# Four graph-attention layers on one core: which unit turns the tiles, and in what order the first and last groups are written

## The chip, the core and the metric

The kernel runs on one core of one Trainium2 chip. A core has five engines that run side by side and wait for each other by semaphores: TensorE (PE; weight loads are listed as PEld), VectorE (DVE), ScalarE (ACT), GpSimd (POOL) and SyncE (SP), which here only issues DMAs. Sixteen DMA engines move data between the chip's memory and the on-chip memory. The metric is the device time of one execution in microseconds; lower is better.

## What is computed

64 graphs of 256 nodes with 256 features pass through four layers. Each layer is an attention over the graph's edges, and after each one `x = layernorm(x + layer(x))`. Cut to what matters here:

```python
# layer 0: 4 heads of 64, masked softmax, output projection, layer norm
attn = softmax(where(adj == 0, NEG, q @ k.T * 64 ** -0.5))
out = layernorm((attn @ v) @ Wo.T + bo) * gamma + beta
# layer 1: 8 heads of 32; q = k = v = layernorm(x)*gamma1+beta1, then an MLP 256-1024-256
x = x + softmax(masked(z @ z.T * 32 ** -0.5)) @ z
out = x + gelu((layernorm(x) * gamma2 + beta2) @ W1 + b1) @ W2 + b2
# layer 2: one head; e = leaky_relu(s1 + s2), softmax over the edges, times h @ W
# layer 3: e_k = leaky_relu((h * a_k) @ h.T) chosen by the edge's type, softmax, times h
```

A matrix product needs the summed index on the partitions, so node-first tiles have to be turned (transposed) before several of the products: `x` before q and k, `z` before layer 1's scores, `yT` before the MLP, `n2` before layer 2 and `n3` before layer 3. Layer 1's head outputs come out feature-first and have to be turned back before they are added to node-first `x`.

## The kernel before, in words

`usual_input` (from L416) computes the usual case; at the end a flag says whether the input allowed it, and the general `any_input` runs only if not. All arithmetic is in f32. The 64 graphs are worked in 32 groups of two. Every group is a set of eleven generators, called threads (`threads_of`, L1066): `a` loads and masks, makes q, k, v, layer 0's scores, exponentials and products (L651); `u0`, `u1`, one for each graph, do the rest of layer 0 (L752); `z0`, `z1` turn z (L791); `b` is layer 1's attention (L798); `w0`, `w1` its sums and second norm (L837); `c` the first product of the MLP with Gelu (L866); `o0`, `o1` the second product and layers 2 and 3 (L911).

A thread is cut into steps by `yield`. `PLACES` gives each step of each thread a place in units of one group's period; group g adds g. The steps of all groups are sorted by place (L1075) and issued in that order, and the class `InOrder` (L432) keeps each engine's instructions in just this order. Engines still run apart and wait only for data and buffers. So the order of the work is written out, engine by engine, and an instruction that waits holds up all that stand behind it on its engine, SyncE's queue of DMAs among them. `prepare` (L992) works out constants from the weights; one of its parts is issued after each step from `PREPARE` = 2 on. As every call goes through the helper `issue`, the profile puts nearly all instructions on its line, L444, and they are told apart by their tiles.

**Turning a tile.** `flipped` (L620) has two ways. With `direct`, four TensorE transposes of 128x128 go into PSUM and ScalarE copies them out. Otherwise `put` (L599) writes the tile to a buffer `rows` in the chip's memory with two DMAs, `get` (L606) reads it back in four DMAs as `blk`, so that 32x32 blocks stand where they belong, and `turn_blocks` (L614) turns each block with one VectorE transpose. Before the change z, yT, n2 and n3 of all groups go by DMA. `x` is also read by DMA as blocks, `turned` (L487), and turned by VectorE. Layer 1's head outputs `oT` are turned by four TensorE transposes for each graph in `thread_w` (`pm<-ident,oT` in the profile).

**Layer 0's sums.** `products` in `thread_a` (L727) multiplies the exponentials with v and, with a matrix of ones, makes the softmax sums `pz`, 128x256: each head's sum of each node stands in 32 equal rows. VectorE takes the reciprocal of the whole tile into `zs`; ScalarE passes over it once more to add the reciprocals up into `r_0`, which the check at the end needs. `thread_u` writes four rows of `zs` (one for each head) to the chip's memory (`lines`), reads them back spread over the partitions (`rr`), multiplies `oT` with them and goes on to the product with `woT`.

The order of loads at the start: adjacency of the first group, its `turned` blocks, `x`; the weights for q, k, v on ScalarE's queue; the others on SyncE's as part of `prepare`.

Of the kernel before, what the change touches and what calls it, by code (L numbers as in the profile page):

```python
# [8 lines left out]
F32 = mybir.dt.float32  # L9
# [28 lines left out]
SCZ = SCB = SCN = True  # L38
B2 = False
BUFS = dict(t=6, q=3, k=2, v=5, y=4, z=5, xb=5, both=4, xn=6, mask=3, e=5, x0=2, turned=1, blk=3, oT=2, zs=2, rr=2, xT=1, qT=1, kT=1)  # L40
PLACES = {
    "a": (0.0000, 0.1609, 0.3936, 0.4188, 1.1456, 1.2085, 1.2135, 1.2684, 1.2684, 1.3083, 1.3187, 1.3922,
        1.4411, 1.4550, 1.5065, 1.5209, 1.5704, 1.6232, 1.7014, 1.7014, 1.7046, 1.7114, 1.7202, 1.7320,
        1.7466,),
    "u0": (1.7845, 1.8009, 1.8519, 1.8867, 1.9096, 1.9241, 1.9842, 1.9890, 2.0092, 2.1939,),
    "u1": (1.8219, 1.8841, 1.9554, 2.0080, 2.0097, 2.0560, 2.0570, 2.0890, 2.1304, 2.1482,),
    "z0": (2.0380, 2.0800, 2.1517, 2.1771,),
    "z1": (2.1482, 2.1622, 2.2237, 2.2465,),
    "b": (2.2092, 2.2292, 2.2314, 2.2463, 2.2634, 2.2658, 2.2687, 2.2708, 2.2708, 2.2724, 2.2924, 2.3032,
        2.3032, 2.3033, 2.3118, 2.3118, 2.3245, 2.3249, 2.3345, 2.3549,),  # L50
    "w0": (2.3066, 2.3129, 2.3245, 2.3779, 2.4390, 2.5803, 2.5997, 2.6786,),
    "w1": (2.4161, 2.4739, 2.4805, 2.4835, 2.6234, 2.6271, 2.6419, 2.7222,),
    "c": (2.7903, 2.8184, 2.8324, 2.9205, 2.9215, 2.9612, 3.0404, 3.0557,),
    "o0": (3.0690, 3.0731, 3.1620, 3.1894, 3.2073, 3.2439, 3.2672, 3.3855, 3.4219, 3.4420, 3.4926, 3.5020,
        3.5298, 3.5520, 3.5620, 3.5786, 3.6006, 3.7170, 3.7358, 3.7614, 3.8702, 3.9115, 3.9399, 3.9768,
        4.0664, 4.2516, 4.2674, 4.2795, 4.2936, 4.3095, 4.3669, 4.3935, 4.6003, 5.1336,),
    "o1": (3.0936, 3.2383, 3.2389, 3.2476, 3.3303, 3.5076, 3.5188, 3.5336, 3.5988, 3.6912, 3.7420, 3.7551,
        3.7936, 3.8172, 3.8298, 3.8317, 3.8389, 3.8773, 3.9738, 3.9793, 4.0267, 4.0708, 4.0708, 4.0809,
        4.1171, 4.5258, 4.5963, 4.6712, 4.6849, 4.7832, 4.8010, 4.9844, 4.9844, 5.1775,),
}  # L60
PREPARE = 2

# [357 lines left out]
def usual_input(ctx: ExitStack, tc: tile.TileContext, a: dict, out: bass.AP, flag: bass.AP):  # L420
# [56 lines left out]
    edges = const.tile([P, B // G], F32, name="edges")  # L477
    r_0 = const.tile([P, B], F32, name="r_0")
    r_3 = const.tile([P, B, QB], F32, name="r_3")
    last = const.tile([P, B, QB], F32, name="last")  # L480
# [6 lines left out]
    def load_x(g):  # L487
        turned = None
        if FX:
            turned = new(io, [P, NC, T // 32, 32], F32, "turned")  # L490
            rows = a["x"][g * G:(g + 1) * G].rearrange("b n d -> (b n) d")
            parts = rows.rearrange("(t i) (c k j) -> k i c t j", i=32, c=NC, j=32)
            for k in range(P // 32):
                for c in range(NC):
                    SP.dma_start(turned[32 * k:32 * k + 32, c], parts[k, :, c])
        x0 = new(io, [P, TB, D], F32, "x0")
        SP.dma_start(x0, a["x"][g * G:(g + 1) * G].rearrange("b (q p) d -> p (b q) d", p=P))
        return x0, turned
# [3 lines left out]
    def load(queue, to, of):  # L502
        if queue:
            queue.dma_start(to, of)
        else:
            later.append((to, of))
# [15 lines left out]

    def load_all(src, name, at=None):

        t = const.tile([P, D], F32, name=name) if at is None else setup[:, at:at + D]
        load(None, t, src.unsqueeze(0).to_broadcast([P, D]))
        return t

    first = load_edges(0), load_x(0)
    wqT = load_rows("L0_gnn_WqT", D, ACT)  # L530
    wkT = load_rows("L0_gnn_WkT", D, ACT)
    bq = load_column(a["L0_gnn_bq"], D, "bq", ACT)
    bk = load_column(a["L0_gnn_bk"], D, "bk", ACT)
    wvT = load_rows("L0_gnn_WvT", D, ACT)
    woT = load_rows("L0_gnn_WoT", D)
    bv = load_column(a["L0_gnn_bv"], D, "bv")
# [5 lines left out]
    load(None, a12, a["L2_gnn_a"].rearrange("(s f) o -> o s f", s=2).to_broadcast([P, 2, D]))  # L542
    beta0 = load_all(a["L0_gnn_beta"], "beta0")
    gamma0 = load_all(a["L0_gnn_gamma"], "gamma0")
# [74 lines left out]

    def flipped(src, direct, name):  # L620

        if direct:
            pt = new(ps_m, [P, QB, NC, P], F32, "pm", 4)
            for q in range(QB):
                for c in range(NC):
                    transpose(pt[:, q, c, :], src[:, q, c * P:(c + 1) * P], ident)
            yield
            dst = new(act, [P, QB, NC, P], F32, "t")
            ACT.copy(dst, pt)
            return dst  # L630
        rows = put(src)
        yield
        blk = get(rows)
        yield
        return turn_blocks(blk)
# [15 lines left out]
    def thread_a(g, s):  # L651
# [18 lines left out]
        xT = new(act, [P, NC, T], F32, "xT")  # L670
        if FX:
            DVE.transpose(xT.rearrange("p c t -> p (c t)"), turned.rearrange("p c t j -> p (c t j)"))
        else:
            pts = []
            for c in range(NC):
                pt = new(ps_m, [P, T], F32, "pm", 4)
                for t in range(TB):
                    transpose(pt[:, t * P:(t + 1) * P], s["x"][:, t, c * P:(c + 1) * P], ident)
                ACT.copy(xT[:, c, :], pt)
# [30 lines left out]
        def scores(i):  # L710
            ps = []
            for c in range(NC):
                p = new(ps_s, [P, 2, QB * N], F32, "ps", 2)
                for kc in range(QB):
                    for h in range(2):
                        r = h * 64
                        matmul(p[:, h, kc * N:(kc + 1) * N], kT[r:r + 64, c, i * N + kc * P:i * N + (kc + 1) * P],
                               qT[r:r + 64, c, i * N:(i + 1) * N], start=True, stop=True)
                ps.append(p)
            yield  # L720
            es = []
            for c in range(NC):
                es.append(exp_of(ps[c], 64 ** -0.5, mask[:, i, :], None, c, 0))
                yield
            return es

        def products(i, es):  # L727
# [6 lines left out]
            pz = new(ps_m, [P, N], F32, "pm", 4)  # L734
            for kc in range(QB):
                for h in range(4):
                    matmul(pz[32 * h:32 * h + 32, :], ones[:, 0:32], es[h // 2][:, h % 2, kc * N:(kc + 1) * N],
                           start=kc == 0, stop=kc == QB - 1)
# [3 lines left out]
            zs = s["zs", i] = new(act, [P, N], F32, "zs")  # L742
            DVE.reciprocal(zs, pz)
            ACT.activation(pz, zs, AF.Copy, accum_out=r_0[:, g * G + i:g * G + i + 1])
            yield
# [6 lines left out]
    def thread_u(g, s, i):  # L752
# [3 lines left out]
        SP.dma_start(lines.rearrange("c h n -> (c h) n"), zs[0:P:32, :])  # L756
        yield
        for h in range(2):
            SP.dma_start(rr[h * 64:h * 64 + 64, :, :], lines[:, h, :].unsqueeze(0).to_broadcast([64, NC, N]))
# [31 lines left out]
    def thread_z(g, s, i):  # L791
        zT = s["zT", i] = yield from flipped(s["z", i], not FZ, "z")
        yield
# [43 lines left out]
    def thread_w(g, s, i):  # L837
        r, oT = s["sums", i], s["o", i]
        DVE.reciprocal(r, r)
        pt = new(ps_m, [P, QB, D], F32, "pm", 4)  # L840
        for q in range(QB):
            for c in range(NC):
                transpose(pt[:, q, c * P:(c + 1) * P], oT[:, c, q * P:(q + 1) * P], ident)
        yield
        x2 = new(act, [P, QB, D], F32, "y")
# [13 lines left out]
        yield  # L859
        yield from flip_to(s, "yT", i, xb, not FY)  # L860

    def flip_to(s, name, i, src, direct):
        s[name, i] = yield from flipped(src, direct, name)
        yield
# [46 lines left out]
    def thread_o(g, s, i):  # L911
# [15 lines left out]

        xT = yield from flipped(x, not FN2, "n2")
        yield
# [25 lines left out]

        xT = yield from flipped(x, not FN3, "n3")
        yield
# [34 lines left out]
    def prepare():  # L992

        for to, of in later[:-2]:
            SP.dma_start(to, of)
        for _ in range(4):
            yield

# [67 lines left out]
    def threads_of(g):  # L1066
# [4 lines left out]
                "o0": thread_o(g, s, 0), "o1": thread_o(g, s, 1)}  # L1071

    preparing = prepare()
    groups = [threads_of(g) for g in range(B // G)]
    plan = sorted((g + t, g, n, k) for g in range(B // G) for n, ts in PLACES.items() for k, t in enumerate(ts))  # L1075
    for turn, (_, g, name, k) in enumerate(plan):
        next(groups[g][name], END)
        if turn >= PREPARE:
            next(preparing, END)
    assert all(next(t, END) == END for ts in groups for t in ts.values())  # L1080

# [52 lines left out]
```

## Time and profile before

| what | us |
|---|---|
| median of 3 runs (lowest to highest) | 2550.32 (2550.2 to 2553.7) |
| the profiled execution | 2552.08 |
| its span | 2550.3 |
| TensorE busy | 2461.3 (97%) |
| VectorE busy | 2013.9 (79%) |
| ScalarE busy | 1604.5 (63%) |
| GpSimd busy | 675.0 (26%) |
| one group's period in the middle (second group's adjacency load to the next, 1499.87 to 1575.69) | 75.8 |

The profile is of one execution. Busy time is the union of an engine's instructions; matmul ends are modelled and neighbours overlap, so what a TensorE instruction costs is best read from start to start. The span is the time from the first to the last instruction of the program; the executed time is a little longer. A line of a group reads: line, engine, operation, output<-inputs, shapes, count, then busy time and mean ns of one, then the idle time of the engine ahead of these instructions and what ended it.

### The profile page before, as it was taken

The numbers are of one execution on the slowest core, as the hardware profiler recorded it, in microseconds if no ns is written. First come the engines' busy times: TensorE is split into PE (matmuls) and PEld (weight loads), VectorE is DVE, ScalarE is ACT, GpSimd is POOL, SyncE is SP. The second block draws the span as 40 slices with busy tenths as digits, with TensorE's granted clock in tenths as the row PEclk, the third lists the DMA queues.
The fourth block names the chain that finished last, engine by engine and source line by source line (L and its number), as shares of the span: only waits on it lengthen the run. The fifth ranks groups of instructions, "written<-read, shape, count | busy, mean of one in ns | idle before, by whom it ended". The sixth has DMA issues, their size and how long they took to land.

```text
span 2550.3 us, 48577 instructions
## 1 busy us (share of the span) xinstructions
PE 2461.3 (97%) x16424; PEld 1834.3 (72%) x16424; DVE 2013.9 (79%) x6060; ACT 1604.5 (63%) x2687; POOL 675.0 (26%) x1807
## 2 busy tenths in 40 slices
PE   5699999999999999999999999999999999999995
PEld 3377777777777777777777777777777777777764
DVE  3677788888888887887888887888878888888764
ACT  2456666676666666666666666667666666666652
POOL 0122222232232222233222232223223223223311
PEclk8799999999999999999999999999999999999987
DMA  5333444444444444444444444444434444443332
GB/s 132 67 86 86 92 100 91 93 100 91 94 99 91 94 99 96 96 92 94 95 96 96 94 92 95 94 92 100 95 90 99 92 96 97 96 92 87 67 71 51
DMA packets 929360, 234.55 MB, mean 92 GB/s; under 512 B 728784, under 2 KB 928720, under 8 KB 929104
## 3 DMA queue, kind: packets, MB, share of 16 engines
q1 hardware_dynamic: 927744, 230.59, 40.6%
q8 instruction: 132, 2.16, 0.4%
q14 instruction: 124, 1.02, 0.1%
q10 hardware_dynamic: 1360, 0.79, 0.1%
HBM read 138.69 MB, written 84.15 MB: 87 GB/s over the span
## 4 chain that ended last, share of the span: by engine, by line
PE 79%; DVE 6%; POOL 6%; ACT 4%; issue 2%; DMA 1%; SPq 1%; POOLq 0%; ACTq 0%; DVEq 0%
PE pm L444 69%; PE ps L444 10%; POOL rstd L444 3%; DVE y L444 3%; DVE st L444 2%; POOL ve L444 2%; ACT L444 2%; ACT z L444 1%; POOL nm L444 1%; ACT hT L444 1%; SPq L444 1%; DVE mv L444 1%; DVE e L444 0%; DMA blk<-rows 0%; DMA L_gnn_W<-in_L_gnn_W 0%
## 5 line engine op out<-in xcount | busy, mean ns | idle before, releaser
L444 POOL TENSOR_SCALAR ve<-mv 128x2 f32<-128x2 f32 x448 | 163.4, 365 | 1750.7 <-DVE mv L444 1208.0
L444 PE MATMUL pm<-L_gnn_W,hT 128*128 128x256 f32 x2048 | 477.9, 384 | 5.3 <-ACT hT L444 5.3
L444 PE MATMUL pm<-t,L_gnn_W 128*128 128x256 f32 x2048 | 463.0, 379 | 1.4 <-DVE t L444 1.4
L444 PEld LDWEIGHTS pm<-L_gnn_W,hT 128*128 128x128 f32 x2048 | 379.6, 190 | 87.7 <-ACT hT L444 25.0
L444 ACT ACTIVATE e<-ps 128x1024 f32<-128x1024 f32 x384 | 374.1, 1018 | 102.8 <-PE ps L444 100.4
L444 PEld LDWEIGHTS pm<-t,L_gnn_W 128*128 128x128 f32 x2048 | 389.1, 190 | 54.9 <-DVE t L444 1.8
L444 DVE SCALAR_TENSOR_TENSOR e<-e,mask 128x256 f32<-128x256 f32 x1024 | 361.1, 419 | 58.8 <-ACT e L444 58.8
L444 POOL TENSOR_TENSOR rstd<-ve,mhalf 128x2 f32<-128x2 f32 (+1 forms) x384 | 305.7, 796 | 31.9
L444 ACT ACTIVATE xn<-y,nm,rstd 128x256 f32<-128x256 f32 x256 | 139.8, 594 | 199.5 <-POOL xn L444 155.0
L444 DVE BATCH_NORM_STATS2 st<-y 128x6 f32<-128x256 f32 x640 | 236.9, 412 | 5.6
L444 ACT ACTIVATE hT<-pm,b 128x512 f32<-128x512 f32 x256 | 167.7, 682 | 51.3 <-PE pm L444 48.9
L444 DVE STREAM_TRANSPOSE t<-blk 128x512 f32<-128x512 f32 x256 | 178.8, 698 | 22.7 <-DMA blk<-rows 22.6
L444 PE MATMUL ps<-t 32*128 32x256 f32 x2048 | 158.2, 405 | 14.3 <-ACT t L444 12.5
L444 ACT ACT_TABLE_LOAD x127 | 162.9, 1283 | 5.7 <-issue 3.5
L444 DVE TENSOR_TENSOR e<-e,mask 128x1024 f32<-128x1024 f32 x128 | 152.1, 1211 | 12.4 <-ACT e L444 12.4
L444 PEld LDWEIGHTS ps<-t 32*128 32x128 f32 x2048 | 101.7, 186 | 67.3 <-ACT t L444 23.1
L444 PE MATMUL pm<-xn,q 128*128 128x257 f32 x512 | 135.6, 389 | 0.0
L444 PE MATMUL pm<-L_gnn_WoT,oT 128*128 128x256 f32 x512 | 125.0, 388 | 9.3 <-DVE oT L444 9.2
L444 PE MATMUL pm<-v,q 128*128 128x260 f32 x512 | 127.4, 393 | 5.1 <-DVE q L444 3.6
L444 PE MATMUL pm<-e,z 128*32 128x256 f32 x2048 | 131.7, 384 | 0.1
L444 ACT COPY v<-pm 128x259 f32<-128x259 f32 (+1 forms) x192 | 84.1, 438 | 75.4 <-PE pm L444 71.4
L444 DVE SCALAR_TENSOR_TENSOR y<-pm,r,xn 128x256 f32<-128x256 f32 x256 | 123.9, 484 | 9.0
(126 smaller groups left out, 4162.3 us busy)
## 6 DMA issues: line engine op xcount, KB each, us to landing
blk<-rows SPq DMA_DIRECT2D x1024, 64.0 KB
rows<-xn SPq DMA_DIRECT2D x256, 128.0 KB
adj<-in_adj SPq DMA_DIRECT2D x32, 512.0 KB
turned<-in_x SPq DMA_DIRECT2D x256, 64.0 KB
x<-in_x SPq DMA_DIRECT2D x32, 512.0 KB
rr<-lines SPq DMA_DIRECT2D x128, 128.0 KB
rows<-z SPq DMA_DIRECT2D x128, 128.0 KB
rows<-xb SPq DMA_DIRECT2D x128, 128.0 KB
```

Source lines behind the costliest of these rows:

```text
L444: ins = call(*args, **kw)
```

## The change

It has four parts.

1. `FO`: `thread_w` writes `oT` to `rows` with two DMAs, reads it back with `get` and turns the blocks with VectorE, in place of TensorE's four transposes. It adds one step to `w0` and `w1`.
2. `SM`: ScalarE only copies `pz` to `zs`; the four rows go to `lines` as before, come back as a 32x32 tile `few`, are inverted there, written out to a second `lines`, and spread from that. The adding up for `r_0` is done on the small tile. It adds three steps to `u0` and `u1`.
3. `DIRECT`: in the first group (0) `x` and `z` are turned by TensorE, and the sums take the old way; in the last (31) `yT`, `n2`, `n3` and the head outputs are turned by TensorE. `x` of the first group is now loaded ahead of its adjacency, and `beta0` on ScalarE's queue.
4. The order: `PLACES` has new numbers throughout; the first 500 and the last 484 of the steps follow two written lists, `FIRST` and `LAST`; the parts of `prepare` are issued after seven named steps.

`PA` is false and changes nothing. `any_input` is as before. The order of each engine moves accordingly; ScalarE's has 65 table loads where it had 127.

```diff
+FO = True
+PA = False
+SM = True
+DIRECT = {0: ('x', 'z', 'sm'), 31: ('yT', 'n2', 'n3', 'o')}
...
-PREPARE = 2
+PREPARE = (8, 16, 30, 60, 75, 85, 95)
+FIRST = (
+    "a0a0a0a0a0a0a0a0a1a1a1a1a1a0a0a0a0a0a0a0a0a0a0a0a0a0a0a0U0U0U0a1a1U0a0a0U0U0u0u0a2a2U0U0U0u0u0u0u0u0U0U0U0u0"
...
-        if FX:
+        if FX and "x" not in DIRECT.get(g, ()):
...
-    first = load_edges(0), load_x(0)
+    x_first = load_x(0)
+    first = load_edges(0), x_first
...
+    beta0 = load_all(a["L0_gnn_beta"], "beta0", queue=ACT)
...
-        if direct:
+        if direct or name in DIRECT.get(g, ()):
...
             ACT.copy(dst, pt)
+            if not direct:
+                yield
             return dst
...
-            DVE.reciprocal(zs, pz)
-            ACT.activation(pz, zs, AF.Copy, accum_out=r_0[:, g * G + i:g * G + i + 1])
+            if SM and "sm" not in DIRECT.get(g, ()):
+                ACT.copy(zs, pz)
+            else:
+                DVE.reciprocal(zs, pz)
+                ACT.activation(pz, zs, AF.Copy, accum_out=r_0[:, g * G + i:g * G + i + 1])
...
+        elif SM:
+            few = new(small, [32, 32], F32, "few", 4)
+            SP.dma_start(few, lines.rearrange("c h (a b) -> (c h a) b", b=32))
+            yield
+            DVE.reciprocal(few, few)
+            ACT.activation(few_out[0:32, :], few, AF.Copy, accum_out=r_0[0:32, g * G + i:g * G + i + 1])
+            yield
+            lines = new(dram, [NC, 2, N], F32, "lines", 4)
+            SP.dma_start(lines.rearrange("c h (a b) -> (c h a) b", b=32), few)
+            yield
...
-        DVE.reciprocal(r, r)
-        pt = new(ps_m, [P, QB, D], F32, "pm", 4)
-        for q in range(QB):
+        if FO and "o" not in DIRECT.get(g, ()):
+            DVE.reciprocal(r, r)
+            rows = new(dram, [QB, NC, P, P], F32, "rows", 8)
             for c in range(NC):
-                transpose(pt[:, q, c * P:(c + 1) * P], oT[:, c, q * P:(q + 1) * P], ident)
-        yield
+                SP.dma_start(rows[:, c].rearrange("q p j -> p q j"), oT[:, c, :].rearrange("p (q j) -> p q j", q=QB))
+            yield
+            blk = get(rows)
+            yield
+            pt = turn_blocks(blk).rearrange("p q c j -> p q (c j)")
...
-        for to, of in later[:-2]:
+        for to, of in later[:3]:
             SP.dma_start(to, of)
-        for _ in range(4):
-            yield
+        yield
+        for to, of in later[3:-2]:
+            SP.dma_start(to, of)
+        yield
...
-    plan = sorted((g + t, g, n, k) for g in range(B // G) for n, ts in PLACES.items() for k, t in enumerate(ts))
-    for turn, (_, g, name, k) in enumerate(plan):
+    plan = [(g, n) for _, g, n in sorted((g + t, g, n) for g in range(B // G) for n, ts in PLACES.items() for t in ts)]
+    head, tail = written(FIRST, 0), written(LAST, B // G - 8)
+    for turn, (g, name) in enumerate(head + plan[len(head):len(plan) - len(tail)] + tail):
         next(groups[g][name], END)
-        if turn >= PREPARE:
+        if turn in PREPARE:
             next(preparing, END)
```

In `FIRST` and `LAST` a letter names the thread (`U`, `u` are `u0`, `u1`; `O`, `o` are `o0`, `o1`, and so on) and the digit the group, counted from 0 and from 24.

## The prediction

> **What bounds the kernel now.** I read the table of windows first, since an average over the span hides stages. Its columns are the stretch, its length, each engine's busy time, then the granted TensorE clock, the DMA share and GB/s.
>
> ```profile
> 0.00:100.00 100.00, 54.55 (x278) 33.22 (x282) 43.74 (x115) 27.78 (x44) 9.77 (x29) 0.76 0.47 112
> 100.00:250.00 150.00, 145.04 (x1017) 103.90 (x1013) 112.75 (x349) 89.74 (x143) 34.07 (x76) 1.00 0.37 81
> 250.00:2300.00 2050.00, 2044.97 (x13854) 1529.62 (x13844) 1690.33 (x5086) 1356.58 (x2272) 569.08 (x1515) 1.00 0.43 95
> 2300.00:2450.00 150.00, 146.78 (x1010) 110.84 (x1009) 123.20 (x383) 94.07 (x158) 42.36 (x115) 0.99 0.34 75
> 2450.00:2551.00 101.00, 69.95 (x280) 56.74 (x279) 43.90 (x129) 36.30 (x72) 19.70 (x74) 0.80 0.25 58
> ```
>
> Between 250 and 2300 us TensorE is idle for 5.0 us in 27 groups, 0.19 us a group; VectorE is 82% busy, ScalarE 66%. There the time is TensorE's work. The rest is at the ends: idle for 45.5 us of the first 100 and 31 us of the last 101, at a clock of 0.76 and 0.80. Next, who TensorE waited for (total, times, longest):
>
> ```profile
> PE pm L444 <- DVE hT L444: 18.9, 1, 18.9
> PE ps L444 <- ACT t L444: 12.5, 1, 12.5
> PE pm L444 <- DVE oT L444: 9.2, 3, 5.3
> PE pm L444 <- ACT t L444: 8.6, 2, 5.0
> ```
>
> The waits of 18.9, 12.5 and 5.3 are single ones in the first group; 5.0 belongs to the last. Third, the groups by form that the change touches (count, busy us, mean ns):
>
> ```profile
> L444 PE MATMUL pm<-ident,oT 128*128 128x128 f32 x256 | 40.5, 280 | 0.3 <-ACT oT L444 0.3
> L444 DVE STREAM_TRANSPOSE t<-blk 128x512 f32<-128x512 f32 x256 | 178.8, 698 | 22.7 <-DMA blk<-rows 22.6
> L444 DVE RECIPROCAL zs<-pm 128x256 f32<-128x256 f32 x64 | 112.5, 1757 | 14.3 <-PE pm L444 14.3
> ```
>
> Last, one turn by DMA in the final chain: it costs 6.4 us from the end of xn (2494.79) to the matmul (2501.19).
>
> ```profile
> 2494.79 1.85 DMA rows<-xn
> ...
> 2498.15 2.15 DMA blk<-rows
> ...
> 2500.42 0.72 DVE t L444
> ...
> 2501.19 2.03 PE pm L444 x8
> ```
>
> **Layer 1's head outputs by DMA.** 62 of 64 graphs lose four TensorE transposes each. The busy row gives 40.5/256 = 0.16 us a transpose, but neighbours overlap: in the timeline four start at 1002.90 and the next matmul at 1003.40, four at 1011.49 and the next at 1011.93. By starts a set costs 0.47 us: 62 x 0.47 = **-29 us**; by busy time it would be -39, which I keep for the range. All of it lies in the TensorE-bound stretch. What is added lies beside it: per graph two writes (0.9 us of issue), four reads (1.92) and one VectorE turn (0.70). SyncE's queue waited some 1290 us of the span (the sum of its waits), so it holds the 62 x 2.8 = 175 us. DMA share rises from 43% to about 50%: a turn is 2560 packets, 62 of them 17% of the 929360.
>
> **Layer 0's sums.** VectorE loses 62 x 1.757 = 109 us of reciprocal. A 128x16 reciprocal takes 0.23 us; 32x32 has twice the elements in a partition, so I take 0.25, bounds 0.23 and 0.44 (1.757/4). With 62 turns VectorE goes down by 50 us net. ScalarE loses the pass over pm with its accumulator read (0.39 + 0.19) and gains a copy of that size and a small pass: nothing. As VectorE and ScalarE are not the bound, this gains nothing directly. The order of ScalarE's instructions also halves the table loads (127 before, 65 after; 1.28 us each, -80 us): slack, no gain either.
>
> **The waits that the change adds** decide the rest. I took TensorE's order in both programs and added up the work written between the producer and the consumer of a chain, against the chain's own length by rows:
> - Sums: copies of oT and zs 0.95, lines 0.55 + 1.34 to landing (85.7/64 in SyncE's waits), small load 0.5 + 1.8 (bounds 1.34 and 2.15), reciprocal 0.25, lines back 1.9, rr 1.23 + 2.3 (issued until 61.5, waited for until 63.8), multiply 0.69: 11.5 us, against 7.9 before. Between the first product's end and WoT stand 13.4 us of TensorE (12.5 before). Two us are left. SyncE waits in order through four transfers; behind it stand the writes of xn and z, which those same chains need.
> - WoT to layer 1's scores: y, statistics, POOL, y, statistics, POOL, z 8.9 (1.7 + 1.6 + 1.4 + 1.0 + 2.1 + 1.1), turn 6.1 (2494.30 to 2500.42) + 0.7, gamma and beta 1.1, handovers 0.7: 17.5 us. TensorE has 17.1 between (W1 2 x 3.45, the other graph's WoT 1.7, W2 2 x 3.45, layer 3's scores 1.3, bias 0.2), where before 22.7 passed (1041.08 to 1063.81) and z's turn ended on the same instant as the score began. So 0.4 us late.
> - Head outputs to W1, second graph: 21 us of chain with two turns (14 before), 23 of TensorE.
> So I charge 0.4 us a group for 29 middle groups, **+12 us**. Bounds: 0 (before it was 0.19), and 2.5, as if one landing more were exposed in each group, +73.
>
> **The first group.** x is issued first and takes the place of adj, which landed at 6.0; TensorE turns it, so no turned blocks, no bv product and no set-up of prepare() stand ahead. adj by about 8.5, two ScalarE passes 2.6, copies 1.1, then q and k cold (6.5 each, as now), evacuation 1.4: scores at about 28 instead of 49.6. VectorE then has the second group's mask ahead of the exponentials' (adjacency turned by 30, so 31.5 + 4.7 = 36, now 56.4); SyncE has twelve loads ahead of lines (41, now 58.5): 17 us gained. z by TensorE: four transposes cold 1.2, copy 0.6, gamma and beta 1.1, handovers 0.2, for 10.1 now (76.9 to 87.0): 7 more. Given back: the new turn and the four transfers in groups 0 and 1, where little other work covers them, about 5. Together **-20 us**, bounds -5 and -27.
>
> **The last group.** The final chain loses two DMA turns: 2 x (6.4 - 1.4) = 10, the 1.4 being four transposes and a copy. yT by TensorE takes away the wait of 2.3 at 2449 and what it costs in clock (wx 3.82 for 1.92, v,q 3.80 for 1.95, wx 3.01 for 1.91): 6. The written order keeps parts of the two groups before to lie in the gaps; I take 1. **-17 us**, bounds -8 and -25. The transposes added by TensorE (24 x 0.12 = 3) lie mostly in idle time: +1.
>
> Sum against the profiled execution (2552.1, its span 2550.3): 2552.1 - 29 + 12 - 20 - 17 + 1 = 2499. The median of the runs is 1.8 lower, so **2498**.
>
> One rule speaks against the change. The Trainium skill, page "VectorE: DVE Perf Modes", in "Rules for kernel authors", sends a 128x128 transpose to TensorE where PSUM will do, and "The three transpose paths" warns that a plain strided DMA for a transpose is 19 times slower than the transposing DMA, which it puts at 1.3 us for bf16. By that a turn of four tiles would wait some 100 us (an estimate, 4 x 19 x 1.3) and the schedule would break. The chain above shows 6.4 us, because the strided reads move 128-byte runs and VectorE turns inside 32x32. The row decides.
>
> **Rivals.**
> - *The waits take the gain back and more* (slower). The place is WoT and layer 1's scores, the price each us a group is 29 us. Without the 12, the terms give 2498 - 12 = 2486; at 2.2 us a group (64) all is gone, from 2.4 on it is slower: 2555 to 2590. For it: a slack of 2 and of -0.4 us, and SyncE in order. Against it: the order before was as tight (score and z at the same instant) and lost 0.19. Chance 0.12.
> - *The ends give little*: the first group's lead is lost because groups 1 and 2 wait for their longer chains, so that only TensorE's saving and some of the tail are left: 2552 - 29 + 20 - 5 - 8 = 2530; 2522 to 2545. Chance 0.13.
> - *Nothing*: the transposes ran beside other TensorE work and VectorE at 82% with five turns a graph becomes the wait; 2545 to 2555. Chance 0.04; against it, VectorE's own work goes down.
> - *More than forecast*: transposes at their busy time and no waits, 2455 to 2470. Chance 0.05.
>
> The forecast (2470 to 2522) keeps 0.66. The range 2470 to 2548 holds it, the second rival and part of the third. About 0.2%, 5 us, is what can be told from no change: faster 0.66 + 0.05 + 0.13 = 0.84, same 0.04, slower 0.12.
>
> **What would show it.** Right: pm<-ident,oT x8 left; the middle stretch at 74.9 + 0.4 us a group for 75.9 (adj to adj), TensorE idle under 1 us a group; first scores of layer 1 near 62; the last chain without DMA. Wrong: TensorE waiting for oT<-rr or ACT t every group by over 1 us; DVE's reciprocal waiting for few; SyncE's waits for lines above 3 us each; the first 250 us idle as now.

## The result, and the profile after

| | before | after |
|---|---|---|
| median of 4 runs each (lowest to highest), us | 2550.7 (2550.2 to 2553.7) | 2579.4 (2572.3 to 2584.8) |
| ratio, 95% interval | | 1.0108 (1.0082 to 1.0134) |
| profiled execution, span | 2550.3 | 2583.0 |
| first output projection (WoT) of group 0 | 64.5 | 45.3 |
| of group 5 | 432.4 | 431.5 |
| of group 30 | 2328.5 | 2384.0 |
| of group 31 | 2404.3 | 2459.7 |
| from there to the end | 146.0 | 123.3 |

The kernel became slower. The profiled execution of after is the slowest of its four (2584.8 us), so its spans lie 4 us further apart than the medians. The lower rows, read from TensorE's timelines, tell where. The first group gains 19.2 us, and the last stretch 22.7. Groups 0 to 5 give 18.3 back. From group 5 to 30 a period takes 78.10 us and not 75.84, which is 56.4 us in 25 groups. -19.2 + 18.3 + 56.4 - 22.7 makes the 32.7 between the spans.

The table of windows of after, with the columns as before:

```profile
0.00:100.00 100.00, 71.07 (x396) 43.23 (x398) 53.86 (x162) 38.57 (x61) 13.11 (x38) 0.78 0.39 101
100.00:250.00 150.00, 142.86 (x949) 103.34 (x947) 106.60 (x326) 80.75 (x139) 34.31 (x79) 0.98 0.45 96
250.00:2300.00 2050.00, 1992.18 (x13260) 1464.61 (x13259) 1597.10 (x4968) 1257.21 (x2208) 623.16 (x1466) 1.00 0.48 105
2300.00:2450.00 150.00, 146.18 (x981) 107.90 (x983) 119.19 (x376) 90.67 (x161) 41.58 (x109) 1.00 0.48 104
2450.00:2583.00 133.00, 116.87 (x646) 93.67 (x638) 83.04 (x284) 69.09 (x132) 36.96 (x117) 0.97 0.22 53
```

TensorE idles 29 us of the first 100 (45 before) and 16 of the last 133 (31 of 101), but 57.8 in the middle, where it was 5.0. VectorE's mean share there went down, 82% to 78%. The waits of TensorE and VectorE in after (total, times, longest):

```profile
DVE t L474 <- DMA blk<-rows: 134.1, 90, 3.0
DVE oT L474 <- DMA rr<-lines: 71.2, 30, 4.7
PE pm L474 <- DVE r L474: 44.3, 37, 2.3
PE ps L474 <- ACT t L474: 14.4, 27, 1.3
```

The first of these rows in before:

```profile
DVE t L444 <- DMA blk<-rows: 22.6, 10, 7.8
```

VectorE now stands three times in each group for the blocks of a turn, where before it hardly ever did. Groups of after, by form:

```profile
L474 PE MATMUL pm<-ident,oT 128*128 128x128 f32 x8 | 1.5, 294 | 0.3 <-ACT oT L474 0.3
L474 DVE STREAM_TRANSPOSE t<-blk 128x512 f32<-128x512 f32 x310 | 214.6, 699 | 137.1 <-DMA blk<-rows 134.1 <-issue 2.8
L474 DVE RECIPROCAL few<-few 32x32 f32<-32x32 f32 x62 | 20.5, 331 | 9.9 <-DMA few<-lines 9.6
L474 PE MATMUL pm<-e,z 128*32 128x256 f32 x2048 | 164.4, 390 | 2.0
```

The last of them in before:

```profile
L444 PE MATMUL pm<-e,z 128*32 128x256 f32 x2048 | 131.7, 384 | 0.1
```

The change does what it says (eight transposes left). But the same 2048 products of e and z are "busy" for 33 us more: a block that starts and then waits for each next piece of e counts as busy. Idle time alone hides this. I therefore also took each block's time from its start to the next block's, less the shortest usual time of its kind, between 600 and 2250 us (22 groups): before loses some 30 us so, after some 102 (what counts as usual moves the first figure by 10 us). The Trainium skill, page "Perfetto Trace Analysis", section "Identifying the Most-Contended Engine", warns that matmul busy time is no good measure of how close a kernel is to its limit, for another reason: pipelined instructions look smaller in a trace than they are. Here it fails the other way, by counting waits as work: TensorE's share is 96% after and 97% before, while the loss grew by some 70 us.

One period of after, TensorE's timeline (start, us, instruction, idle before and releaser). A product is called by its inputs: wx is layer 2's product with W, e,z layer 1's exponentials times z, v,q layer 2's weights times its values.

```profile
1099.02 1.07 PE L474 MATMUL pm<-e,z 128*32 128x256 f32 x16
1100.02 1.17 PE L474 MATMUL ps<-t 32*128 32x256 f32 x16
1102.07 2.02 PE L474 MATMUL pm<-wx,t 128*128 128x259 f32 x8 [0.88 <-DVE r L474]
1103.92 3.59 PE L474 MATMUL pm<-xT,L_gnn_WqT 128*128 128x512 f32 x8
1107.45 3.15 PE L474 MATMUL pm<-e,z 128*32 128x256 f32 x32
```

The same stretch on VectorE:

```profile
1098.46 1.22 DVE L474 SCALAR_TENSOR_TENSOR mask<-adjT,adjb 128x1024 bf16<-128x1024 bf16 x1
...
1101.30 0.71 DVE L474 STREAM_TRANSPOSE t<-blk 128x512 f32<-128x512 f32 x1 [1.61 <-DMA blk<-rows]
...
1102.50 1.24 DVE L474 STREAM_TRANSPOSE xT<-turned 128x1024 f32<-128x1024 f32 x1
...
1104.23 0.41 DVE L474 SCALAR_TENSOR_TENSOR e<-e,mask 128x256 f32<-128x256 f32 x1
```

and on SyncE:

```profile
1087.39 4.21 SPq L474 DMA_DIRECT2D turned<-in_x  x8
1091.64 0.49 SPq L474 DMA_DIRECT2D x<-in_x  x1
1092.23 0.97 SPq L474 DMA_DIRECT2D rows<-xn  x2
1096.86 1.92 SPq L474 DMA_DIRECT2D blk<-rows  x4
```

Read upwards: the write of the second norm (`rows<-xn`) stands behind the next group's x, 1 MB in nine DMAs, and can be read back only 4.6 us after its issue. VectorE stands 1.61 us for it with the turn of x and the masks of layer 1's last exponentials behind it. So wx starts 0.88 us late, and the block e,z takes 3.15 us where it needs 1.93. Other places wait less: layer 1's scores under 0.6 us in most groups, and WoT 1.01 us in this period, but over 0.1 us in only 8 of 27 groups (8.5 us in all between 250 and 2300 us).

### The profile page after: what moved, and what is told of

It reads as the page before. It is cut to its first block, busy times and chain, and to the rows that moved or that the text cites. A ratio compares the mean times of both kernels' runs of the same rounds, so it can differ in the third digit from the quotient of the medians.

```text
span 2583.0 us, 49347 instructions
## 1 busy us (share of the span) xinstructions
PE 2469.2 (96%) x16216; PEld 1812.7 (70%) x16216; DVE 1959.8 (76%) x6113; ACT 1536.3 (59%) x2697; POOL 749.1 (29%) x1808
## 3 DMA queue, kind: packets, MB, share of 16 engines
q14 instruction: 132, 1.08, 0.1%
## 4 chain that ended last, share of the span: by engine, by line
PE 49%; DVE 21%; DMA 11%; POOL 6%; SPq 5%; ACT 4%; issue 3%; DVEq 0%; POOLq 0%; ACTq 0%
PE pm L474 43%; DVE e L474 7%; PE ps L474 6%; SPq L474 5%; DMA blk<-rows 5%; DVE y L474 4%; POOL rstd L474 3%; DVE st L474 3%; DMA rows<-oT 2%; POOL ve L474 2%; DVE t L474 2%; ACT xn L474 1%; DVE xT L474 1%; POOL nm L474 1%; DMA rr<-lines 1%
## 5 line engine op out<-in xcount | busy, mean ns | idle before, releaser
L474 POOL TENSOR_SCALAR ve<-mv 128x2 f32<-128x2 f32 x448 | 164.4, 367 | 1724.3 <-DVE mv L474 1607.5
L474 POOL TENSOR_TENSOR rstd<-ve,mhalf 128x2 f32<-128x2 f32 (+1 forms) x384 | 331.9, 864 | 32.0
L474 DVE STREAM_TRANSPOSE t<-blk 128x512 f32<-128x512 f32 x310 | 214.6, 699 | 137.1 <-DMA blk<-rows 134.1
L474 PE MATMUL ps<-t 32*128 32x256 f32 x2048 | 153.9, 406 | 17.1 <-ACT t L474 14.4
L474 PE MATMUL pm<-wx,t 128*128 128x259 f32 x512 | 130.1, 397 | 38.0 <-DVE r L474 35.6
L474 PE MATMUL pm<-e,z 128*32 128x256 f32 x2048 | 164.4, 390 | 2.0
L474 ACT ACTIVATE z<-y,nm,rstd 128x256 f32<-128x256 f32 x128 | 69.8, 592 | 135.0 <-POOL nm L474 127.1
L474 PE MATMUL pm<-L_gnn_WoT,oT 128*128 128x256 f32 x512 | 125.2, 389 | 18.3 <-DVE oT L474 9.8
L474 PEld LDWEIGHTS pm<-wx,t 128*128 128x128 f32 x512 | 96.7, 195 | 65.0 <-DVE r L474 46.8
L474 PEld LDWEIGHTS pm<-e,z 128*32 128x32 f32 x2048 | 64.5, 110 | 99.0 <-DVE e L474 42.7
```

The costliest lines, as they stand in the source:

```text
L474: ins = call(*args, **kw)
```

## The experiments: undoing parts of the change

Every ratio below is to before in the same session (medians 2551.2 to 2553.8). Theory A: the added transfers are what TensorE waits for. Theory B: the new order of the middle itself leaves too little between its steps. Theory C: the added traffic lengthens every landing.

**Sums the old way.** In after:

```diff
-DIRECT = {0: ('x', 'z', 'sm'), 31: ('yT', 'n2', 'n3', 'o')}
+DIRECT = {g: ('sm',) for g in range(32)}
+DIRECT[0] += ('x', 'z')
+DIRECT[31] += ('yT', 'n2', 'n3', 'o')
```

> The changed kernel, but layer 0's sums go the old way in all groups (the whole tile inverted, two transfers instead of four); the steps and the written order stay. Theory A, the added transfers are what TensorE waits for: the product with WoT starts at once, about 1.0 us a group less (the wait at WoT), and what that lateness pushed on behind it; 2540 to 2555 us for 2579. Theory B, the new order itself leaves too little between steps, whatever the transfers: 2572 or more. Theory C, the added traffic makes every landing longer: a small part, 2565 to 2572, with shorter landings of blk.

Measured: 2616.7 us, ratio 1.0255 (1.0238 to 1.0272), 37 us slower than after, though two transfers for each graph are gone. **Heads by TensorE** (`('o',)` in place of `('sm',)`):

> The changed kernel, but layer 1's head outputs are turned by TensorE in all groups; the steps and the order stay. TensorE gets its 0.47 us a graph back, 29 us. Theory A: what the turn cost in waits (SyncE's queue, the wait at wx of 0.9 us a group, part of the products e,z) goes, so 2565 to 2585. Theory B: only the 29 us are seen, about 2605. Theory C: less traffic, landings of blk and rr shorter by several tenths, 2570 to 2590.

Measured: 2588.5, 1.0151 (1.0134 to 1.0168): 9 us slower than after, a difference that the noise leaves wide (the two intervals meet at 1.0134). The two profiled executions took the same time (2584.7 and 2584.8 us) and have the same period (78.17 and 78.10), so they don't show it. TensorE gets 29 us of transposes back and only 9 are seen: some 20 us of waits went with the transfers, which is nearer to theory A's range than to B's 2605. **Both the old way**, the order and the ends as in after:

> The changed kernel's order, steps, first and last group, with both the sums and the head outputs in the old way in all groups. Theory A: the middle comes back to the 75.9 us a group of before and the ends keep what they gained (about 30 us by the windows): 2515 to 2535. Theory B: the middle stays at 78 or more with TensorE idle 1.5 us a group or more: 2570 or more.

Measured: 2622.7, 1.0287 (1.027 to 1.0305). Without any of the added transfers the same two stalls are there. The write of the second norm stands behind the same 1 MB and is read back 4.6 us after its issue, and the products e,z are busy for 150.5 us (131.7 in before, 164.4 in after):

```profile
1096.98 0.97 SPq L476 DMA_DIRECT2D rows<-xn  x2
1101.57 1.92 SPq L476 DMA_DIRECT2D blk<-rows  x4
```

```profile
L476 PE MATMUL pm<-e,z 128*32 128x256 f32 x2048 | 150.5, 387 | 1.6
```

**The ends alone**: before with its own order, the first and last group's turns by TensorE, x loaded first, no written lists:

> The kernel before with one part of the change alone: x loaded first, x and z of the first group and yT, n2, n3 of the last turned by TensorE; places and order as before. By the prediction's terms 10 + 6 us in the last group and, as prepare() still stands ahead of the first products, some 7 us in the first (z): 2525 to 2535. Rival: the ends gain only through the written orders, since without them the turned tiles wait for other things: 2543 to 2550.

Measured: 2551.7, 0.9999 (0.999 to 1.0009). The turns by TensorE alone gain nearly nothing: layer 1's first scores start at 87.1 (87.0 in before, 60.1 in after), and the last stretch, from WoT of group 31 to the end, takes 144.1 us (146.0 and 123.3). So the ends gain through the written orders, as the rival said.

Theory A falls as the main cause: with all the added transfers gone the kernel is 43 us slower than after. For the heads alone it holds in part, by the 20 us above. C falls with the trace of the run with both old ways: the late landing is there without the added traffic. B is left, with the new ways making good a part of it.

## The experiments: the order of before

**The written ends round the old middle.** After with the old ways and the old `PLACES`; the steps that the written lists don't name follow in the old order:

```diff
-    for turn, (g, name) in enumerate(head + plan[len(head):len(plan) - len(tail)] + tail):
+    middle = list(plan)
+    for step in head:
+        middle.remove(step)
+    middle.reverse()
+    for step in tail:
+        middle.remove(step)
+    middle.reverse()
+    for turn, (g, name) in enumerate(head + middle + tail):
```

> Old ways in all groups (sums, heads), the middle in the order of before, but the first 500 and last 484 steps as written in after, with the turns of the ends by TensorE. In after the first output projection came 19 us earlier and the stretch from the last group's projection to the end was 23 us shorter, but groups 0 to 5 took 18 us longer. Order theory (the middle's order is what costs): the period is 75.8 us again and the ends keep 20 to 42 us, 2508 to 2532. Rival (the lead of the first group is lost whatever follows, and the tail's gain is only work pushed into the middle): 2545 to 2555.

Measured: 2545.9, 0.9971 (0.9959 to 0.9984). The run with both old ways differs from this one by the middle's order alone: 2622.7 - 2545.9 = **77 us is the price of the new middle order with the old ways**, for which that order was not laid out. The timelines agree: from group 5 to 29 the run with both old ways falls 77 us further behind before, while this one keeps before's period. Its ends gain little: the first projection comes at 45.8, but group 5's at 440.9 (432.4 in before). Of the lead, 9 us are lost between groups 0 and 1, inside the written list, and 18 us between groups 2 and 4, where the two orders join.

**Sums by 32x32 in the order of before**, with the added steps at 1.7230 to 1.8600:

> The kernel before, with its order, and only layer 0's sums inverted as 32x32 by way of the chip's memory, in all groups. The first graph's output projection stands 12.6 us behind the first graph's sums in the written places, and the chain took 14.4 us in the trace of after. Wait theory: 1 to 3 us in each of 32 groups, 2583 to 2645. Order theory: in an order where VectorE has room the new way neither gains nor loses, 2545 to 2560.

Measured: 2637.6, 1.033 (1.0312 to 1.0347); period 78.48. TensorE's timeline:

```profile
1551.62 1.97 PE L444 MATMUL pm<-L_gnn_WoT,oT 128*128 128x256 f32 x8 [1.91 <-DVE oT L444]
```

The wait theory holds here: the chain, 14.4 us in after, doesn't fit into 12.6, and WoT waits 1.2 to 2.7 us in 26 groups between 250 and 2300 us, 1.6 on average. That is the larger part of the 2.6 us by which the period grew; the rest was not taken apart.

**Heads by DMA in the order of before**, the added steps placed by me:

> The kernel before, with its order, and only layer 1's heads turned by DMA and VectorE (62 and 2 more graphs, all 64); w0 and w1 get one step more, and the turn has 8 us between its first write and its product, all ahead of the step of scaling that stood 10 us later anyway. Order theory (the loss lies in the new order of the middle, not in the transfers): TensorE loses 64 x 0.47 us, so 2522 to 2530. Transfer theory (what is sent through the chip's memory is waited for): 2560 or more. Third: heads by DMA are worth 9 us wherever they stand, as between the kernel after and the one with heads by TensorE: 2540 to 2546.

Measured: 3007.1, 1.1778 (1.1758 to 1.1797). **The same with the written ends**:

> As the run with the old middle and the written ends, and layer 1's heads by DMA in groups 0 to 30. Order theory: the sum of the two, 2480 to 2505, which would be faster than both kernels. Transfer theory: 2560 or more.

Measured: 2935.5, 1.1492 (1.1473 to 1.1512). Neither theory had this; by the trace it comes from where I put the steps, and no run has other places for all 64 sets. SyncE's timeline of the first of the two:

```profile
1551.27 1.72 SPq L444 DMA_DIRECT2D rows<-oT  x2
1553.35 5.29 SPq L444 DMA_TRANSPOSE adjT<-adjb  x4
1558.81 2.04 SPq L444 DMA_DIRECT2D blk<-rows  x4
1560.90 4.20 SPq L444 DMA_DIRECT2D turned<-in_x  x8
1565.15 0.49 SPq L444 DMA_DIRECT2D x<-in_x  x1
1565.68 1.02 SPq L444 DMA_DIRECT2D rows<-xn  x2
```

The read back of the second graph's heads stands behind the adjacency's transposes, VectorE stands 7.07 us for it, and the write of the norm for layer 2 comes 24.7 us after the group's first copy of heads, where it came 11.1 us after it in before. TensorE then waits 8.86 us for v,q in this group, 256 us in 31 times over the run, and wx waits for another 93. A read back put behind a transfer of 5 us thus stands in a chain that costs TensorE more than those 5 us in every group.

**The first graph's heads alone**, with x's load moved out of the way (`a` step 3 from 0.4188 to 1.0010) and w0 at 2.4000, 2.4100, 2.4150, 2.4155, 2.4160, 2.4500:

> The kernel before, with its order, and layer 1's heads of the first graph of each group alone turned by DMA and VectorE; the load of x and its turned blocks goes behind the next group's adjacency load, out of the way of the added write and read, and the steps of w0 stand where their data are ready by the trace of before. The second graph keeps its transposes by TensorE. If a set of four transposes is worth 0.47 us wherever the added chain is hidden: 32 x 0.47 = 15 us, 2533 to 2542. If the added transfers can't be hidden in this order: 2560 or more.

Measured: 2576.9, 1.0097 (1.008 to 1.0114). **Mended** (statistics at 2.4425, behind layer 2's v):

> As the run with the first graph's heads by DMA in the order of before, with the norm's statistics of w0 (VectorE and GpSimd) placed behind layer 2's v. In that run v,q waited 0.89 us in every group for a small write of GpSimd that stood behind those statistics on GpSimd's queue. In-order theory: this wait goes, and the 0.47 us of a set of transposes shows, 32 x 0.47 = 15 us off the kernel before: 2533 to 2542. Rival (the added transfers cost it elsewhere): 2550 or more.

Measured: 2563.8, 1.0037 (1.0024 to 1.005). **With the written ends too**:

> As the mended run, with the first 500 and last 484 steps as written in after and the ends' turns by TensorE (7 us off, with the old ways in all groups). In-order theory: 2520 to 2536, faster than both kernels. Rival: the join of the two orders takes the 7 us, 2540 or more.

Measured: 2552.7, 1.0001 (0.9992 to 1.001). The mended kernel got back 13 of the 25 us, but the rival held. The wait is not GpSimd's, as I had it; it went from 0.89 to 0.51 us in each group, and `nm`, which the profile names, is no input of v,q. TensorE and VectorE in the first of the three:

```profile
1560.59 1.77 PE L444 MATMUL pm<-v,q 128*128 128x260 f32 x7 [0.89 <-POOL nm L444]
```

```profile
1551.83 0.66 DVE L444 STREAM_TRANSPOSE t<-blk 128x512 f32<-128x512 f32 x1
...
1558.72 0.99 DVE L444 TENSOR_SCALAR q<-pm,ex 128x256 f32<-128x256 f32 x2
1559.75 0.69 DVE L444 TENSOR_TENSOR q<-q,mask 128x512 f32<-128x512 f32 x1
```

The same q in before:

```profile
1546.69 0.99 DVE L444 TENSOR_SCALAR q<-pm,ex 128x256 f32<-128x256 f32 x2 [0.45 <-PE pm L444]
```

v,q starts 0.15 us after the q that it reads, and VectorE has no gap from 1549.62 to 1560.44, the added turn and what follows it among that; in before it had 0.45 us to spare just ahead of q. The transposes cost TensorE 0.47 us; the turn costs VectorE 0.66, and in this stretch TensorE waits for VectorE. How much of the loss is the turn's is not shown: these runs also move x's load, and with w0 some 2.4 us of VectorE's work (the sums' scaling and its statistics) into this stretch, and no run makes these moves without the turn.

## The experiments: moving single steps in after

**The small reciprocal ahead of q** (`u0`: 1.37897, 1.41437 become 1.32900, 1.35400; only VectorE's order and the accumulator's place on ScalarE change):

> The kernel after with two places of the first graph's sums changed: VectorE inverts the small tile ahead of layer 3's q (1.7 us), behind which it stood while its load had landed. In-order theory: the sums come 1.7 us earlier and WoT's wait of 0.7 to 1.0 us in each middle group goes, 2552 to 2562. Rival (the DMA hops alone set the chain's end): under 0.2 us a group, 2573 to 2585.

Measured: 2566.0, 1.0052 (1.0036 to 1.0069), 13 us less than after; of WoT's 8.5 us of waits between 250 and 2300 us 0.3 are left. The gain is a little under what I expected, and far from the rival. **The load of x behind the turn of the second norm** (`a` step 3: 0.79867 becomes 0.81950), and then **both moves**:

> The kernel after with one place changed: the step that loads the next group's x and its turned blocks (nine DMAs, 4.7 us of SyncE's time, 1 MB) goes behind the write and the read back of the first graph's second norm, where it stood just ahead of them. In the trace of after that write was issued 1.7 us after its data were ready and landed 3.7 us after it was issued (1.5 in before), VectorE stood 1.6 us for its blocks at 1101, and the product wx 0.9 us, and the last exponentials of layer 1 came 1.2 us late for e,z. In-order theory (a late turn holds up SyncE's queue and then VectorE's, and TensorE waits for what stands behind): wx and e,z lose their stalls, 1 to 2 us less in each of 28 middle groups, 2523 to 2552. Rival (the transfers' own length or the load on the DMA engines): no change, 2570 to 2585.

> The kernel after with the moves of both runs. In-order theory: the sum of the two, 2500 to 2535, which would be faster than the kernel before. If the two stalls stand on one chain, so that one move only lets the other wait show: no faster than the better of the two by over 8 us.

Measured: 2613.1, 1.0239 (1.0222 to 1.0256), and 2576.9, 1.0097 (1.008 to 1.0113). wx no longer waits at that point, but `xT<-turned` now waits for its blocks (21.4 us in 26 times), the second wx waits up to 2 us, and e,z still takes 3.09 us. The move passed the wait on.

**Two VectorE steps past the late turn**, with the reciprocal's move:

```diff
-    "a": (... 0.86691, 0.89274,      "o0": (... 3.88819, 3.88820,
+    "a": (... 0.86691, 0.87200,      "o0": (... 3.87210, 3.88820,
```

> The kernel after with the small tile's inversion ahead of q (as in the run that gave 13 us) and two of VectorE's steps, the turn of the next group's x and one of layer 3's divisions (1.9 us together), ahead of the turn of the second norm, for whose blocks VectorE stands 1.6 us idle in after with the last exponentials' masks behind it. TensorE's order and all DMAs stay. In-order theory: the masks end 1.2 to 1.9 us earlier, the stall of e,z (1.2 us a group) goes: 28 groups, 2528 to 2545, at or under the kernel before. Rival (the late product is bound by the exponentials on ScalarE or by the late landing itself): 2560 to 2568.

Measured: 2543.6, 0.9963 (0.995 to 0.9977): **36 us under after, and the first kernel with the new middle order under before** (the old middle with the written ends had 2545.9). 22 of the 36 us come with the two VectorE steps. TensorE's timeline:

```profile
1084.70 2.02 PE L474 MATMUL pm<-wx,t 128*128 128x259 f32 x8 [0.91 <-DVE r L474]
1086.56 3.59 PE L474 MATMUL pm<-xT,L_gnn_WqT 128*128 128x512 f32 x8
1090.08 1.93 PE L474 MATMUL pm<-e,z 128*32 128x256 f32 x32
```

The block e,z is back at 1.93 us; neither TensorE's order nor a DMA was touched. This shows the mechanism for that stall. wx waits as in after (37 us between 250 and 2300 us, 34 in after).

**Heads by TensorE in this kernel**:

> The kernel with the three moves, and layer 1's heads turned by TensorE in all groups (in after that was worth 9 us). If the heads by DMA are worth 62 sets x 0.47 us once VectorE no longer stands behind the late turn: 29 us slower, 2565 to 2578. If the transposes had gaps to run in, or the added turn costs VectorE what TensorE gains: 2540 to 2556.

Measured: 2561.8, 1.0034 (1.0021 to 1.0046): the heads by DMA are worth 18 us here (9 in after, with the noise said there), 11 less than 62 x 0.47.

**The plain load of x moved away** (behind the adjacency's transposes; the turned blocks stay):

> The kernel with the three moves, and the plain load of x (0.5 MB in one DMA) issued some 20 us earlier, behind the transposes of the adjacency; the eight loads of the turned blocks stay. In after, the write of the second norm issued just behind both loads landed 3.7 us later, against 1.5 in before. Landing theory: with half of the bytes ahead of it gone it lands 1 to 2 us earlier, wx's wait of 0.9 to 1.3 us in every group goes, 28 groups: 2512 to 2530. Rival (the write waits for SyncE or for the blocks' own loads): under 0.3 us a group, 2535 to 2548.

Measured: 2542.6, 0.9964 (0.9952 to 0.9976), no gain over the three moves. SyncE's timeline:

```profile
1062.04 2.09 SPq L474 DMA_DIRECT2D turned<-in_x  x4
1064.22 0.95 SPq L474 DMA_DIRECT2D rows<-xn  x2
1066.84 1.91 SPq L474 DMA_DIRECT2D blk<-rows  x4
```

The landing theory was right of the write (2.6 us from issue to the read behind it, not 4.6) and wrong of the gain: wx still waited 0.91 us, now with VectorE busy ahead of the turn. **The turn put first**, ahead of mask, xT and a division, in the kernel with x's load moved (`o0` step 7: 2.87237 becomes 2.86600):

> The kernel with the three moves and the split loads of x, and the turn of the second norm of each group's first graph three VectorE instructions earlier (ahead of the mask, the turn of the next x and a division, 3.0 us), as its blocks now land before VectorE reaches the mask. In-order theory: wx's wait of 0.91 us in every middle group goes and the masks of the last exponentials end when they did: 25 us less, 2510 to 2526, some 1.3% faster than the kernel before. Rival (the landing is still the bound): 2536 to 2548.

Measured: 2560.6, 1.0041 (1.0027 to 1.0054), 18 us slower. TensorE:

```profile
1313.70 2.02 PE L474 MATMUL pm<-wx,t 128*128 128x259 f32 x8
1317.07 3.70 PE L474 MATMUL pm<-xT,L_gnn_WqT 128*128 128x512 f32 x8 [1.35 <-ACT v L474]
```

and VectorE:

```profile
1312.09 0.71 DVE L474 STREAM_TRANSPOSE t<-blk 128x512 f32<-128x512 f32 x1 [1.08 <-DMA blk<-rows]
1312.73 1.18 DVE L474 SCALAR_TENSOR_TENSOR mask<-adjT,adjb 128x1024 bf16<-128x1024 bf16 x1
1313.84 1.24 DVE L474 STREAM_TRANSPOSE xT<-turned 128x1024 f32<-128x1024 f32 x1
```

and ScalarE:

```profile
1316.65 0.64 ACT L474 COPY v<-pm 128x259 f32<-128x259 f32 x2
```

wx starts at once, but Wq, the next product, waits 1.35 us instead, in 26 groups. It does not wait for xT: VectorE idled 1.08 us ahead of the turn, yet xT was ready at 1315.08, before wx ended at 1315.72. By the profile Wq waits for ScalarE's first copy of wx's result, done at 1317.0, which stands on ScalarE behind two exponentials and the next norm. In the run with x's load moved, Wq started at 1076.60 right behind wx, ahead of that copy at 1076.71; why it waits for the copy here was not taken apart. So the wait was passed on once more, this time to ScalarE, and how to free wx stays open.

## Why the prediction was wrong, point by point

**The step that failed is the charge for the waits the change adds: 0.4 us a group, +12 us.** Expected was a period of 74.9 + 0.4; measured were 78.10 in the profiled execution, 2.8 us a group more than that. Three things were left out of it.
- I set each chain's bare length against TensorE's work between its ends, and named WoT and layer 1's scores as the tight places. They wait, but for some 0.7 us of the loss a group, start to start, and WoT in 8 of 27 groups only. The larger part, some 2.3 us (25 us ahead of wx and 25.6 at e,z in 22 groups), is at places that I did not name. There the added length is not a chain's own: VectorE stands in its written order behind a turn that has not landed. I checked that VectorE's share goes down, which was true and said nothing of the stretch.
- The chain's rows were taken short. The reciprocal of 32x32 took 0.33 us (0.25 taken, bounds 0.23 and 0.44); the lines back landed 2.76 us after their issue at 1135 (1.9 taken), rr 2.47 us after its (2.3), and the reciprocal stood behind q for some 2 us. In that period this makes 14.4 us for 11.5, against 13.4 of TensorE.
- The new order was priced only by the chains that it lengthens. With the old ways it costs 77 us, and it holds both stalls without any added transfer: the next x's 1 MB stands just ahead of the second norm's write, and the last exponentials' masks behind its turn. How much room an order leaves on VectorE is a term of its own, and it was missing.

**Heads by DMA, -29.** TensorE's starts are gone as counted, but the gain was about 9 us in after, 18 with the three moves, and less than nothing in the order of before with the places that I gave the steps. The 0.70 us of VectorE that I put "beside it" is on the path where VectorE has no gap.

**Sums, no direct gain.** Wrong in after's order, where they are worth 37 us: with the 1.76 us reciprocal of the whole tile back, TensorE waits `PE pm <- ACT pm` 29 times, 19.7 us in all, for ScalarE's pass over the sums that follows it. What the rest of the 37 us is was not taken apart. In the order of before, with the places that I gave the steps, they cost 85 us. The same change gains or costs by the order that it stands in.

**The first group, -20.** The size was right: first scores of layer 1 at 60.1 (62 predicted), first projection 19.2 us earlier. Two sums are a little off as written: the terms up to layer 0's first scores make 26.6 us, not 28 (25.0 measured), and 17 + 7 - 5 is 19. That the lead stays was wrong; it was gone by group 5. The second rival said so, but not why: with the old ways it is lost as well. **The last group, -17:** 22.7 us, within its bounds, but with luck. I gave 16 of the 17 to the turns by TensorE and 1 to the written order. With the turns alone, in the order of before, the last stretch is 1.9 us shorter, so nearly all of the 22.7 needs the written order.

**The rivals.** The slower side came true (2555 to 2590, chance 0.12), and above the price of 2.4 us a group that I gave for it (0.4 + 2.8), but mostly at other places than I gave. The period and TensorE's idle time showed that the forecast was wrong. The signs that I named for it did not show as named: layer 1's scores wait for t by about 0.5 us, WoT by over 1 us in few groups, the small reciprocal waits for `few` 9 times in all, SyncE's waits for lines are 1 to 1.3 us each, and TensorE idles 36 us of the first 250 where it was 50.

The rule that the prediction weighed, 128x128 transposes to TensorE, fits the runs in the order of before (no gain from the DMA way) and does not fit the kernel with three moves (18 us for the DMA way). Neither the 19 times nor the 100 us worked out from it appeared. The Trainium skill, page "VectorE: DVE Perf Modes", section "The three transpose paths", states that factor for a large innermost stride of the destination; whether the 128-byte runs are what avoids it no run here tests.

What stays open: wx's wait, some 37 us even with the three moves, was moved twice and never removed. The second product of the MLP and the scores behind it (17 us in 22 groups of after) were not taken apart; a loss of this kind is there in before too, where the longest of these blocks takes 4.05 us from start to start. An order made anew for VectorE's full stretches was not tried.

## What to carry to other kernels

In a kernel whose order is written out, moving work from the bounding engine to one that is "76% busy" is safe only where that engine has gaps; look at its timeline at the very place, and at who stands behind the moved instruction in its queue. Price an order by the bounding engine's loss from start to start, not by idle time, and price the order apart from the change that comes with it. A lead won at the start of a pipeline has to be followed into the middle: here it was gone by group 5 with either middle order.

## What the runs showed of the hardware

A write issued on SyncE's queue right behind 1 MB of loads could be read back 4.6 us after its issue, in after and in the run with both old ways; with half of that gone it took 2.6 us. The Trainium skill, page "DMA: Bandwidth & Descriptors", section "Queues, rings and completion order", has each DMA engine take its descriptors in the order of the ring; the two figures agree with it, and don't tell it from a mere sharing of the engines' time. And a reciprocal of 32x32 costs 0.33 us where 128x16, half as many elements in a partition, cost 0.23: a small tile is cheap, not free.
